# A row LSTM: output gates written to the next row's place of h, the odd cell tanh and product over 128 rows, and no copy of x rows into PSUM

## The chip, the cores and the metric

The kernel runs on one core of a Trainium2 chip. The metric is the device time of one execution, in microseconds (us); for the kernel before it is the median of three runs.

## The reference

The input `x` is (8, 96, 128, 128): 8 images, 96 channels, 128 rows of 128 pixels. It is normalised over groups of 3 channels (mean and variance over 3 x 128 x 128), and the normalised image goes through a convolutional LSTM that walks down the rows:

```python
its = conv(X, W_is * mask, 1x3) + b_is        # 4*96 outputs for each pixel, all rows at once
def step(carry, row_in):                       # one row of 8 images x 128 pixels
    h, c = carry
    gates = conv1d(h, W_ss, 3 taps) + b_ss + row_in
    f, i, o = sigmoid(...), sigmoid(...), sigmoid(...); g = tanh(...)   # 96 channels each
    c_new = f * c + i * g
    h_new = o * tanh(c_new)
    return (h_new, c_new), h_new
out = x + hs
```

The mask leaves two of the three taps of `W_is` (the pixel to the left and, for part of the channels, the pixel itself). Everything is 32-bit float. Row r needs h and c of row r - 1, so the 128 rows are a chain.

## The kernel before

Until about 155 us the kernel reads all of x once for the sums of the normalisation, while the first rows start. The rest, which this document is about, is the walk down the rows.

**Half-steps.** The 8 images are two groups of four (s = 0 and 1). A *half-step* `n` is one row of one group; the groups alternate, so the work of two half-steps overlaps. There are 256 half-steps; 252 of them are written by one string, `PERIOD`, that lists the work of all engines in order. The scheduler is switched off for TensorE (PE), ScalarE (ACT), VectorE (DVE) and GpSimd (POOL): each engine runs its own part of that string in that order, and waits with semaphores where it needs something. A name in the string is an operation, the letter behind it a bank or a pixel kind, `'` the half-step before, `+` the one behind.

**Pixels.** Even pixels (part `a` in the string) and odd ones (`b`) are kept apart: a tile has 64 even and 64 odd pixels for each of four images, 256 columns each. `hx[s][i][:, r]` holds a row: partitions 0 to 95 are h of the row before (the convolution's input), partitions 96 to 127 are 32 channels of the normalised x of this row, so one matmul over 128 partitions does both. A convolution of three taps over pairs of pixels is written with fewer products, from four operands: the sum `vs` of even and odd pixels (`total`, L750), their difference `vf` (`difference`, L754), and the differences of neighbours `vo` (`shifted_odd`, L764) and `ve` (`shifted_even`, in the tile `te`, L760).

**Banks and lanes.** A half-step has three PSUM banks of 128 x 512: A (forget gate, and a third of g), B (input gate, and a third of the output gate), C (two thirds of the output gate and two of g). Columns 0 to 255 are first the part `m` that both pixel kinds share, columns 256 to 511 the part that differs. When the shared part is complete, ScalarE copies it with the bias to SBUF (`copy`, L629); VectorE makes the even gates `m + differing` (`even`, L635) and the odd ones `m - differing` (`odd`, L639), and the rest of the products (`vo`, `te`) is added on top. Every product is cut into two matmuls over 64 partitions (two *lanes*, partitions 0 to 63 and 64 to 127), which run beside each other; where both lanes write one bank, an empty instruction on TensorE (`Lanes.wait`) lets the second wait for the first. TensorE shows two instructions for a 32-bit matmul.

**The gates and h.** ScalarE makes tanh of g (`tanh`, L644), sigmoid of the gates (`sigmoid`, L665), and the last third of the output gate (`last_output_gate`, `o2`, L670), which lies in partitions 96 to 127 of bank B. Output gates go to a tile `o` of 96 x 512. VectorE multiplies input gate and g for odd pixels (`gated`, L684; GpSimd does the even ones, L682), forget gate and c (`forget`, L675), and adds both to c (`cell`, L697). ScalarE takes tanh of c (`cell_tanh`, L705) to PSUM: odd pixels to bank B, even ones to bank C. VectorE multiplies with `o` (`output`, L714): the even h goes to its place in `hx` of the next row; the odd h stays in PSUM, in bank B's columns 256 to 511, partitions 0 to 95. Three things read the odd h there: `total` and `difference` of the next row, `residual` (L776, out = x + h), and a copy on ScalarE to `hx` (`keep_odd`, `co`, L725), from which GpSimd makes `vo`. Since `total` and `difference` need 128 partitions, ScalarE first copies the 32 odd x rows of the next row out of `hx` into partitions 96 to 127 of the same columns (`shared_odd`, `uo`, L730):

```python
self.kept["uo"] = nc.scalar.activation(
    self.odd_output[C:P], hx[self.s][i][C:P, r, 1, :, 1 : J + 1], AF.Identity
)
```

PSUM is tracked by whole banks; where two instructions touch different partitions of a bank, `apart` tells the framework that they need not wait for each other.

## Time and profile before

| | |
|---|---|
| median of 3 runs | 1937.43 us (1936.2 to 1940.31) |
| the profiled execution | 1935.68 us, its span 1933.9 us |
| mean granted TensorE clock | 0.990 |
| busy share of the span: PE, ACT, DVE, POOL | 97%, 86%, 81%, 81% |
| the chain that ended last | PE 92%, DMA 3%, DVE 2%, ACT 1%, POOL 1% |
| from 190 to 1904 us | 15663 matmul instructions in 1714 us |

An execution's time holds its span and what lies around it. A line of the profile names the source line, the engine, the operation, and output<-inputs by the program's names; `x2` behind it means that two equal ones were merged; what stands in brackets is the idle time ahead and who ended it. An instruction can start before the one ahead on its engine has ended, so durations of neighbours overlap.

### The profile page before, as it was taken

How to read it: one execution, taken by the hardware profiler on the slowest of the kernel's cores; microseconds unless marked ns; L12 is line 12 of the kernel's file. 1: busy time of each engine (PE TensorE's matmuls, PEld its weight loads, DVE VectorE, ACT ScalarE, POOL GpSimd, SP SyncE). 2: the span in 40 equal slices, each digit the busy share in tenths (PEclk: the TensorE clock that was granted, in tenths of full speed). 3: DMA queues.
4: the chain of work that ended last, by engine and by line, in shares of the span. 5: the costliest groups of instructions: out<-in, count | busy, mean ns of one | idle time of the engine just before them, and what ended most of it. 6: DMA issues, size and time to landing. Idle time of an engine off the chain costs nothing.

```text
span 1933.9 us, 45949 instructions
## 1 busy us (share of the span) xinstructions
PE 1876.7 (97%) x16440; PEld 1760.7 (91%) x16440; DVE 1565.7 (81%) x4024; ACT 1661.7 (86%) x3939; POOL 1566.5 (81%) x2172
## 2 busy tenths in 40 slices
PE   4789999999999999999999999999999999999998
PEld 1458999999999999999999999999999999999996
DVE  5887888888888888888888888888888888888886
ACT  6578888888888888888888888888888888888887
POOL 4348988888888888888888888888888888888852
PEclk8899999999999999999999999999999999999999
DMA  9995434433443443444344434443443444345311
GB/s 404 406 324 115 109 90 121 123 102 97 123 109 93 112 126 102 103 117 118 91 107 121 112 100 110 121 102 94 121 122 95 105 121 110 89 118 126 91 29 44
DMA packets 110292, 242.82 MB, mean 126 GB/s; under 512 B 6833, under 2 KB 16369, under 8 KB 104049
## 3 DMA queue, kind: packets, MB, share of 16 engines
q1 hardware_dynamic: 110064, 239.89, 45.1%
q8 instruction: 130, 2.13, 0.5%
q14 instruction: 98, 0.79, 0.1%
HBM read 181.34 MB, written 50.33 MB: 120 GB/s over the span
## 4 chain that ended last, share of the span: by engine, by line
PE 92%; DMA 3%; DVE 2%; ACT 1%; POOL 1%; issue 0%; SPq 0%; DVEq 0%; POOLq 0%; ACTq 0%
PE ps L553 92%; DMA x<-in_x_dram 2%; DVE bst L1229 1%; DMA te<-in_x_dram 1%; POOL xw L354 0%; ACT g L644 0%; POOL xs L375 0%; ACT ps L665 0%; PE rows L225 0%; POOL xs L371 0%; PE pv L308 0%; ACT o L670 0%; POOL g L682 0%; SPq L1216 0%; ACT hx L273 0%
## 5 line engine op out<-in xcount | busy, mean ns | idle before, releaser
L553 PE MATMUL ps<-te,wl 64*128 64x256 f32 (+1 forms) x3042 | 924.3, 384 | 0.2
L553 PE MATMUL ps<-vf,wm 64*128 64x256 f32 (+1 forms) x3046 | 780.5, 376 | 0.1
L553 PE MATMUL ps<-vo,wl 64*128 64x256 f32 (+1 forms) x3042 | 736.1, 384 | 2.5 <-DVE ps L639 2.4
L553 PE MATMUL ps<-xs,wx 64*128 64x256 f32 (+1 forms) x3080 | 731.1, 377 | 3.4 <-POOL xs L371 2.3
L553 PE MATMUL ps<-vs,wm 64*128 64x256 f32 (+1 forms) x3046 | 676.8, 376 | 2.9 <-DVE vs L750 2.8
L635 DVE TENSOR_TENSOR ps<-m,ps 128x256 f32<-128x256 f32 x768 | 323.4, 421 | 266.7 <-ACT m L629 266.6
L553 PEld LDWEIGHTS ps<-te,wl 64*128 64x128 f32 (+1 forms) x3042 | 511.9, 185 | 29.9 <-PE ps L553 1.4
L553 PEld LDWEIGHTS ps<-vo,wl 64*128 64x128 f32 (+1 forms) x3042 | 495.5, 186 | 13.9 <-issue 4.0
L553 PEld LDWEIGHTS ps<-xs,wx 64*128 64x128 f32 x3080 | 492.3, 187 | 15.3 <-POOL xs L371 3.2
L553 PEld LDWEIGHTS ps<-vs,wm 64*128 64x128 f32 (+1 forms) x3046 | 452.9, 187 | 14.3 <-DVE vs L750 4.2
L553 PEld LDWEIGHTS ps<-vf,wm 64*128 64x128 f32 (+1 forms) x3046 | 446.5, 185 | 16.1 <-PE ps L553 0.9
L629 ACT ACTIVATE m<-ps,wl 128x256 f32<-128x256 f32 x766 | 359.9, 470 | 23.2 <-PE ps L553 10.4
L644 ACT ACTIVATE g<-ps 32x512 f32<-32x512 f32 x765 | 317.8, 447 | 55.1 <-PE ps L553 39.8
L639 DVE TENSOR_TENSOR ps<-m,ps 128x256 f32<-128x256 f32 x768 | 325.5, 424 | 17.6
L553 PE MATMUL ps<-xs,wt 64*128 64x256 f32 x1012 | 299.2, 376 | 1.4 <-DVE ps L639 1.4
L682 POOL TENSOR_TENSOR g<-i,g 96x256 f32<-96x256 f32 x251 | 182.2, 726 | 144.3 <-ACT g L644 143.7
L375 POOL TENSOR_TENSOR xs<-xw 128x512 f32<-128x512 f32 (+1 forms) x254 | 293.2, 1155 | 0.1
L665 ACT ACTIVATE ps<-ps 96x512 f32<-96x512 f32 (+1 forms) x512 | 243.2, 475 | 34.9 <-PE ps L553 12.0
L354 POOL TENSOR_SCALAR xw<-xr,rstd,nmr 128x512 f32<-128x512 f32 (+1 forms) x267 | 208.2, 781 | 37.3 <-DVE nmr L346 13.0
L705 ACT ACTIVATE ps<-c 96x256 f32<-96x256 f32 x512 | 193.2, 378 | 39.7 <-DVE c L697 4.6
L354 POOL TENSOR_SCALAR hx<-x,rstd,nmr 32x512 f32<-32x512 f32 x248 | 201.6, 813 | 25.7
L697 DVE TENSOR_TENSOR c<-ps,g 96x256 f32<-96x256 f32 (+1 forms) x507 | 211.2, 417 | 10.1 <-POOL g L682 1.3
(133 smaller groups left out, 2608.5 us busy)
## 6 DMA issues: line engine op xcount, KB each, us to landing
xr<-in_x_dram SPq DMA_DIRECT2D x124, 512.0 KB, 6.6
x<-in_x_dram SPq DMA_DIRECT2D x62, 768.0 KB, 5.2
out_dram<-x SPq DMA_DIRECT2D x62, 768.0 KB, 4.6
x<-in_x_dram SPq DMA_DIRECT2D x16, 1024.0 KB, 11.0
x<-in_x_dram SPq DMA_DIRECT2D x62, 256.0 KB, 3.0
xs<-in_x_dram SPq DMA_DIRECT2D x15, 1024.0 KB, 11.1
te<-in_x_dram SPq DMA_DIRECT2D x8, 1024.0 KB, 10.3
hx<-in_x_dram SPq DMA_DIRECT2D x8, 1024.0 KB, 9.6
```

The source lines that it names most:

```text
L354: return engine.tensor_scalar(dst, src, scale, shift, ALU.mult, ALU.add)
L375: return engine.tensor_sub(differences, strided(xw[:, 0, :], 0, [(W + 1, n), (J + 1, 2), (1, J)]), strided(xw[:, 0, :], J, [(W + 1, n), (0 ...
L553: made = nc.tensor.matmul(self.ps[a][:, bass.ts(half, HB)][:, cols], weights[rows, bass.ts(a, P)], rhs[rows, cols], start=new, stop=False, ...
L629: made = nc.scalar.activation(self.m1[a], m1, AF.Identity, bias=column)
L635: nc.vector.tensor_add(self.ps[a][:, 0:HB], self.m1[a], self.ps[a][:, HB:])
L639: nc.vector.tensor_sub(hi, self.m1[a], hi)
L644: made = nc.scalar.activation(self.part(g, lo, hi, t), self.part(ps, lo, hi, t), AF.Tanh)
L665: made = nc.scalar.activation(to, gate, AF.Sigmoid)
L682: nc.gpsimd.tensor_mul(to, i, g)
L697: nc.vector.tensor_add(c, f, g)
L705: nc.scalar.activation(th, self.part(self.c, lo, hi, t), AF.Tanh)
L1229: nc.vector.bn_stats(bst[:, done, :], xc[:, bass.ts(j, SN)])
```

## The change

- `sigmoid` of bank C and `last_output_gate` write the output gates to the next row's place of h in `hx` (`self.h`, partitions 0 to 95, even and odd pixels) instead of the tile `o`, which is gone. The product for even pixels replaces the gate in place; `keep_odd` later writes the odd h over the odd gate.
- c becomes 128 partitions high; partitions 96 to 127 of its odd half are filled once with 30.0, whose tanh is 1. The odd `cell_tanh` and the odd `output` run over 128 partitions. There the second factor is what lies in partitions 96 to 127 of the next row's `hx`: the normalised x. So the product leaves h and x beside each other in PSUM.
- `shared_odd` is gone, and so is its `uo'` in `PERIOD`, in `LAST` and in the half-step 1.
- The bookkeeping of `apart` becomes a general rule (`touch`). The dependency that held the copy of bank B behind a product of bank C (`"2C"`) is gone. `do` takes one more mark in names that `PERIOD` doesn't use; `LAST` names one residual more, of a half-step that is done by then.

```diff
-    cs = [const.tile([C, 2, BH, J], F32, tag=f"c{s}", name=f"c{s}") for s in range(NH)]
+    cs = [const.tile([P, 2, BH, J], F32, tag=f"c{s}", name=f"c{s}") for s in range(NH)]
...
+        nc.gpsimd.memset(cs[s][C:P, 1], 30.0)
...
+            nxt = hx[self.s][(self.row + 1) // R % 2][:, (self.row + 1) % R]
+            self.beside = strided(nxt[:, 0, 0, :], 0, [(BH * JP + 1, 2), (JP, BH), (1, J)])
+            self.h = self.beside[0:C]
+            self.wide = P if self.banked and self.row + 1 < NT else C
...
+        def touch(self, a, made, lo, hi):
+
+            before = self.touched.setdefault(a, [])
+            same = made.ins.engine == E.Activation
+            for other, l, h, at in before:
+                if (h <= lo or l >= hi) and (
+                    other.ins.engine != made.ins.engine or same and at < len(activations) - 1
+                ):
+                    apart(made, other)
+            before.append((made, lo, hi, len(activations)))
+            return made
...
-                made = nc.scalar.activation(self.m1[a], m1, AF.Identity, bias=column)
-                if a == order["B"] and "2C" in self.kept:
-                    follow(made, self.kept["2C"], "the products of this bank end ahead of it")
+                activate(self.m1[a], m1, AF.Identity, bias=column)
...
             elif a == order["C"]:
-                to = self.part(self.o[0:C2], lo, hi, t)
+                to = self.h[0:C2, :, lo:hi] if t is None else self.h[0:C2, t, lo:hi]
...
         def last_output_gate(self):
-            self.kept["o2"] = nc.scalar.activation(self.o[C2:C], self.ps[1][C:P], AF.Sigmoid)
+            made = activate(self.h[C2:C], self.part(self.ps[1][C:P], 0, BH), AF.Sigmoid)
+            self.touch(1, made, C, P)
...
         def tanh_of(self, t):
-            return self.ps[(2, 1)[t]][0:C]
+            return self.ps[(2, 1)[t]][0 : self.wide if t else C]
...
             for t in range(2) if t is None else (t,):
                 th = self.part(self.tanh_of(t), lo, hi, t)
-                nc.scalar.activation(th, self.part(self.c, lo, hi, t), AF.Tanh)
+                of = self.c_or_one[0 : self.wide] if t else self.c
+                made = activate(th, self.part(of, lo, hi, t), AF.Tanh)
+                self.touch((2, 1)[t], made, 0, self.wide if t else C)
...
             for t in range(2) if t is None else (t,):
-                o, th = (self.part(ap, lo, hi, t) for ap in (self.o, self.tanh_of(t)))
-                to = th if t == 1 and self.banked else self.h[:, t, lo:hi]
-                made = nc.vector.tensor_mul(to, o, th)
-                if t == 1 and self.banked:
-                    self.kept["oub"] = made
-                    apart(made, self.kept.get("uo"))
+                th, wide = self.part(self.tanh_of(t), lo, hi, t), self.wide if t else C
+                o = self.beside[0:wide, t, lo:hi]
+                to = th if t == 1 and self.banked else o
+                self.touch((2, 1)[t], nc.vector.tensor_mul(to, o, th), 0, wide)
...
-        def shared_odd(self):
-            if self.banked and self.row + 1 < NT:
-                i, r = (self.row + 1) // R % 2, (self.row + 1) % R
-                self.kept["uo"] = nc.scalar.activation(
-                    self.odd_output[C:P], hx[self.s][i][C:P, r, 1, :, 1 : J + 1], AF.Identity
-                )
-                apart(self.kept["uo"], self.kept.get("gtb"), self.kept.get("oub"))
...
-        "ceb' 1C> rea'' loB thb' cea' QA+< hiB tha' 3A> 0B< oub' uo' oua' 0A> EB< QC+> cpC S' "
+        "ceb' 1C> rea'' loB thb' cea' QA+< hiB tha' 3A> 0B< oub' oua' 0A> EB< QC+> cpC S' "
```

On TensorE and on the DMA queue of SyncE the order and the waits stay as they were in all 252 half-steps; GpSimd has the two fills more, at the start. VectorE runs the same operations in the same order. Here it is from the odd difference of bank B to that of bank C, in row 61 of group 1 with bank C of row 63 of group 0 (`ps1` is bank B, `ps2` bank C, `hx11` the place of the next row). Before:

```order
L639 TENSOR_TENSOR ps1_0_63_11856<-m1_0_63_11942,ps1_0_63_11856 128x256 [waits DVE_49]
L714 TENSOR_TENSOR ps1_1_61_11766<-o_1_61_11915,ps1_1_61_11766 96x256 [waits Activation_49]
L714 TENSOR_TENSOR hx11_70<-o_1_61_11915,ps2_1_61_11794 96x4x64 [waits Activation_49]
L750 TENSOR_TENSOR vs_1_62_11980<-hx11_70,ps1_1_61_11766 128x256 [waits DVE_49,Activation_49]
L754 TENSOR_TENSOR vf_1_62_11982<-ps1_1_61_11766,hx11_70 128x256
L635 TENSOR_TENSOR ps2_0_63_11884<-m2_0_63_11978,ps2_0_63_11884 128x256 [waits Activation_49]
L639 TENSOR_TENSOR ps2_0_63_11884<-m2_0_63_11978,ps2_0_63_11884 128x256 [waits DVE_49]
```

And now:

```order
L662 TENSOR_TENSOR ps1_0_63_11613<-m1_0_63_11697,ps1_0_63_11613 128x256 [waits DVE_49]
L729 TENSOR_TENSOR ps1_1_61_11525<-hx11_70,ps1_1_61_11525 128x256 [waits Activation_49]
L729 TENSOR_TENSOR hx11_70<-hx11_70,ps2_1_61_11552 96x4x64 [waits Activation_49]
L755 TENSOR_TENSOR vs_1_62_11734<-hx11_70,ps1_1_61_11525 128x256 [waits DVE_49]
L759 TENSOR_TENSOR vf_1_62_11736<-ps1_1_61_11525,hx11_70 128x256
L658 TENSOR_TENSOR ps2_0_63_11640<-m2_0_63_11732,ps2_0_63_11640 128x256 [waits Activation_49]
L662 TENSOR_TENSOR ps2_0_63_11640<-m2_0_63_11732,ps2_0_63_11640 128x256 [waits DVE_49]
```

The two products read `hx11` where they read `o`, the first over 128 partitions; the sum behind them (L750, now L755) waits for VectorE alone, no longer for VectorE and ScalarE.

ScalarE in the same half-step, from the output gates of bank C to the last third of the output gate of the next half-step. Before:

```order
L665 ACTIVATE o_1_61_11915<-ps2_1_61_11794 64x512
L705 ACTIVATE ps1_1_61_11766<-c1_82 96x256 [waits DVE_49]
L705 ACTIVATE ps2_1_61_11794<-c1_82 96x256 [waits DVE_49,Activation_49]
L730 ACTIVATE ps1_1_61_11766<-hx11_70 32x256
L629 ACTIVATE m2_0_63_11978<-ps2_0_63_11884,wl_61 128x256 [waits PE_49]
L665 ACTIVATE ps0_0_63_11853<-ps0_0_63_11853 96x512 [waits PE_49]
L725 ACTIVATE hx11_70<-ps1_1_61_11766 96x4x64 [waits DVE_49,Activation_49]
L644 ACTIVATE g_0_63_11998<-ps0_0_63_11853 32x512 [waits Activation_49,Pool_49]
L670 ACTIVATE o_0_63_12004<-ps1_0_63_11856 32x512 [waits PE_49]
L665 ACTIVATE i_0_63_12008<-ps1_0_63_11856 96x256
```

And now (all activations are issued by one helper, so they share a line):

```order
L520 ACTIVATE hx11_70<-ps2_1_61_11552 64x2x4x64
L520 ACTIVATE ps1_1_61_11525<-c1_82 128x256 [waits DVE_49]
L520 ACTIVATE ps2_1_61_11552<-c1_82 96x256 [waits DVE_49,Activation_49]
L520 ACTIVATE m2_0_63_11732<-ps2_0_63_11640,wl_61 128x256 [waits PE_49]
L520 ACTIVATE ps0_0_63_11610<-ps0_0_63_11610 96x512 [waits PE_49]
L520 ACTIVATE hx11_70<-ps1_1_61_11525 96x4x64 [waits DVE_49]
L520 ACTIVATE g_0_63_11752<-ps0_0_63_11610 32x512 [waits Pool_49]
L520 ACTIVATE hx00_67<-ps1_0_63_11613 32x2x4x64 [waits PE_49]
L520 ACTIVATE i_0_63_11761<-ps1_0_63_11613 96x256
```

The copy of the x rows (32x256, L730) is gone, and the copy of `m2`, the shared part of bank C, follows the two tanh directly. The gates go to `hx11` and `hx00`, in four runs of 64 for each pixel kind. The copy of the odd h and the tanh behind it have each lost the wait on ScalarE itself.

More of the change, by code (lines that the diff above doesn't have):

```diff
@@ L513, with activate @@
     whole = slice(0, P)
+    activations = []
+    def activate(*args, **kwargs):
+        activations.append(nc.scalar.activation(*args, **kwargs))
+        return activations[-1]
     class HalfStep:
@@ L520, in __init__ @@
             i, r = self.row // R % 2, self.row % R
-            self.ps, self.m1, self.done, self.gates, self.outputs = {}, {}, set(), None, None
+            self.ps, self.m1, self.done, self.gates = {}, {}, set(), None
             self.banked = self.n >= 1
@@ L643, in tanh @@
             g, ps = self.g[to], self.ps[a][of]
-            made = nc.scalar.activation(self.part(g, lo, hi, t), self.part(ps, lo, hi, t), AF.Tanh)
-            if a == order["A"]:
-                self.kept["taA"] = made
-        @property
-        def o(self):
-            if self.outputs is None:
-                self.outputs = self.tile("o")
-            return self.outputs
+            made = activate(self.part(g, lo, hi, t), self.part(ps, lo, hi, t), AF.Tanh)
+            self.touch(a, made, of.start, of.stop)
         def sigmoid(self, a, lo=0, hi=BH, t=None):
@@ L661, in sigmoid @@
             elif a == order["C"]:
-                to = self.part(self.o[0:C2], lo, hi, t)
+                to = self.h[0:C2, :, lo:hi] if t is None else self.h[0:C2, t, lo:hi]
             else:
                 to = gate
-            made = nc.scalar.activation(to, gate, AF.Sigmoid)
+            made = activate(to, gate, AF.Sigmoid)
+            self.touch(a, made, 0, C2 if a == order["C"] else C)
             if a == order["C"] and self.banked and (self.row + 1) % R == 0 and self.s in widened:
@@ L674, in forget @@
             if self.row > 0:
-                apart(nc.vector.tensor_mul(f, f, c), self.kept.get("taA"))
+                self.touch(0, nc.vector.tensor_mul(f, f, c), 0, C)
         def gated(self, lo=0, hi=BH, t=None):
@@ L775, in residual @@
                 engine = nc.gpsimd if t == 0 and self.n < last else nc.vector
-                engine.tensor_add(xo[:, t], xo[:, t], h)
+                made = engine.tensor_add(xo[:, t], xo[:, t], h)
+                if t == 1 and self.banked:
+                    self.touch(1, made, 0, C)
                 return
@@ L915, in do @@
         for name in names.split():
-            if name == "U":
-                prepare(n - 1, name)
-                continue
-            if name[0] == "W":
-                prepare(n - 1 + name.count("+") - name.count("'"), name.strip("W+'"))
+            if name[0] in "UW":
+                ahead = name.count("+") + 2 * name.count("*") - name.count("'")
+                prepare(n - 1 + ahead, name.strip("W+*'"))
                 continue
@@ L1292 @@
     finish(0)
[L1293 removed]
+    do(1, "gt th 0+A 3+A 0+B 3+B 0+C 3+C ou co F S D0 D1 re")
     finish(1)
```

23 lines of the change are left out of this document (9 added, 14 removed), and 2 rows, old and new, of the table PARTS.

## The prediction

> **What bounds the kernel now.** I read the page's busy shares first, then stretches of the span, then the timelines of one half-step, and the waits last. The page says that TensorE is busy nearly always:
>
> ```profile
> PE 1876.7 (97%) x16440; PEld 1760.7 (91%) x16440; DVE 1565.7 (81%) x4024; ACT 1661.7 (86%) x3939; POOL 1566.5 (81%) x2172
> ```
>
> That hides the question. The busy times by stretch answer it. The columns are the stretch, its length, then for PE, PEld, DVE, ACT and POOL the busy time and the number of instructions, then the granted clock:
>
> ```profile
> 190.00:1904.00 1714.00, 1714.00 (x15663) 1653.73 (x15663) 1403.51 (x3670) 1510.87 (x3671) 1459.35 (x1939) 1.00 0.42 106
> 1000.25:1003.70 3.45, 3.45 (x35) 3.38 (x33) 3.31 (x11) 3.11 (x9) 3.13 (x5) 1.00 0.72 142
> 1003.70:1007.25 3.55, 3.55 (x35) 3.38 (x33) 2.44 (x7) 3.07 (x9) 2.90 (x5) 1.00 0.18 37
> ```
>
> In the middle 1714 us the matmul row has no idle time at all, and the clock is 1.00. The next two rows are the two halves of one half-step. Each has 35 matmuls, of which three were still running from before, so 32 begin in each; but 32 beginnings take 3.45 us in the first half and 3.55 us in the second. A half-step has 64 of them and takes 7.00 us; at the pace of the first half it would take 2 x 3.45 = 6.90. So TensorE loses 0.10 us somewhere in each half-step, although no view calls it idle. With 15663 / 64 = 244.7 half-steps in the stretch (1714 / 244.7 = 7.004 us each), all that could be won here is about 244.7 x 0.10 = 24 us.
>
> The Trainium skill ("Trainium Kernel Development and Optimization", Performance Expectations) calls matmul busy time a bad metric and weight-load busy time a good one. By the first there is nothing to win. By the second there is: the PEld column has 1653.73 of 1714. The trace sides with the second.
>
> TensorE's timeline shows where the loss is:
>
> ```profile
> 1003.71 0.80 PE L553 MATMUL ps<-vo,wl 64*128 64x256 f32 x4
> ...
> 1004.34 0.38 PE L553 MATMUL ps<-te,wl 64*128 64x256 f32 x1
> 1004.36 0.38 PE L553 MATMUL ps<-vf,wm 64*128 64x256 f32 x1
> ...
> 1006.39 0.70 PE L553 MATMUL ps<-xs,wx 64*128 64x256 f32 x4
> ```
>
> Matmuls come from two row groups in turn, which run beside each other; I call them lanes. Four in a row at full pace take 0.70 us (the last row). The four odd products of bank C from 1003.71 take 0.80, and behind them the two lanes start 0.02 us apart (1004.34, 1004.36) where they would alternate by 0.108 (3.45 / 32). One lane came 0.10 late. Its products need VectorE's difference for bank C, so I go there:
>
> ```profile
> 1001.36 0.42 DVE L714 TENSOR_TENSOR ps<-o,ps 96x256 f32<-96x256 f32 x1
> 1001.69 0.41 DVE L714 TENSOR_TENSOR hx<-o,ps 96x256 f32<-96x256 f32 x1
> 1002.20 0.42 DVE L750 TENSOR_TENSOR vs<-hx,ps 128x256 f32<-128x256 f32 x1
> 1002.54 0.42 DVE L754 TENSOR_TENSOR vf<-ps,hx 128x256 f32<-128x256 f32 x1
> 1002.87 0.42 DVE L635 TENSOR_TENSOR ps<-m,ps 128x256 f32<-128x256 f32 x1
> 1003.32 0.43 DVE L639 TENSOR_TENSOR ps<-m,ps 128x256 f32<-128x256 f32 x1
> ...
> 1005.72 0.43 DVE L635 TENSOR_TENSOR ps<-m,ps 128x256 f32<-128x256 f32 x1 [1.05 <-ACT m L629]
> 1006.18 0.43 DVE L639 TENSOR_TENSOR ps<-m,ps 128x256 f32<-128x256 f32 x1
> 1006.57 0.42 DVE L684 TENSOR_TENSOR g<-ps,g 96x256 f32<-96x256 f32 x1
> 1007.02 0.42 DVE L697 TENSOR_TENSOR c<-ps,g 96x256 f32<-96x256 f32 x1
> ```
>
> The `L639` at 1003.32 is that difference. It ends at 1003.75, and the late lane starts behind it. From 1006.57 on VectorE does not rest until the next one at 1010.32 (the same rows 7.00 us later): an instruction that needs nothing from the one ahead starts 0.33 us after it (1001.36 to 1001.69), one that waits for the result ahead starts 0.03 after that ends (1005.72 + 0.43 = 6.15, then 6.18; 1006.57 + 0.42 = 6.99, then 7.02; 1002.87 + 0.42 = 3.29, then 3.32). One breaks the pattern: `L750`, the sum of even and odd pixels, starts at 1002.20, while the product ahead ended at 1001.69 + 0.41 = 2.10. That is 0.10 instead of 0.03.
>
> ScalarE in the same half-step (`L730` is the copy of x rows into PSUM):
>
> ```profile
> 1000.68 0.90 ACT L705 ACTIVATE ps<-c 96x256 f32<-96x256 f32 x2
> 1001.61 0.38 ACT L730 ACTIVATE ps<-hx 32x256 f32<-32x256 f32 x1
> 1002.01 0.48 ACT L629 ACTIVATE m<-ps,wl 128x256 f32<-128x256 f32 x1
> 1002.61 0.57 ACT L665 ACTIVATE ps<-ps 96x512 f32<-96x512 f32 x1
> 1003.10 0.37 ACT L725 ACTIVATE hx<-ps 96x256 f32<-96x256 f32 x1
> ...
> 1004.34 0.59 ACT L670 ACTIVATE o<-ps 32x512 f32<-32x512 f32 x1 [0.24 <-PE ps L553]
> ...
> 1006.16 0.65 ACT L644 ACTIVATE g<-ps 64x256 f32<-64x256 f32 x2 [0.20 <-PE ps L553]
> 1006.83 0.47 ACT L629 ACTIVATE m<-ps,wl 128x256 f32<-128x256 f32 x1
> ```
>
> ```profile
> DVE ps L635 <- ACT m L629: 258.1, 244, 1.1
> ...
> ACT o L670 <- PE ps L553: 59.0, 241, 0.2
> ...
> ACT g L644 <- PE ps L553: 38.1, 184, 0.3
> ```
>
> Two chains lead into VectorE's stretch. **Chain 1:** bank C's last products release the tanh `L644` at 1006.16 (idle 0.20 before it, for PE); its first half lasts 0.38, and VectorE's `L684` starts behind it at 1006.57. This chain closes on itself: late difference for C, late lane, late tanh, `L684`, next difference. From 1003.75 to 1010.75 it is 7.00 us, and I find no link with slack. **Chain 2:** bank B's products release `L670` at 1004.34, ScalarE makes the copy that VectorE's `L635` at 1005.72 waits for (the first line of the waits: 258.1 us in 244 pieces), and `L639` at 1006.18 would let `L684` start at 6.18 + 0.33 = 6.51. It starts at 6.57, so chain 2 has 0.06 us of slack. It closes over two half-steps: bank B's last products run in the other lane, which waits for the late one only behind them, so they feel a delay one half-step later.
>
> **The change, part by part.** *The copy of x rows goes.* It is `L730`, 0.38 us and 0.02 us of turnaround per half-step (1001.61 to 1002.01): 252 x 0.40 = 101 us of ScalarE. On its own that is worth nothing. The copy `L629` behind it moves up at most to 1001.61, but `L635`, which needs it at 1002.87, has time since 2.01 + 0.48 = 2.49. The sigmoid `L665` at 1002.61 has 0.12 us of idle time ahead and waits for TensorE, so it stays, and with it everything on ScalarE until `L670`, which waits again.
>
> *What goes with it is a wait.* The sum `L750` waits now for VectorE's product and for ScalarE's copy; after the change for the product alone. I take the row 0.03 (three dependent starts with one wait) for its new gap, so it starts 0.10 - 0.03 = 0.07 us earlier, and the difference for C behind it too. The bounds are 0, if the 0.10 has another cause, and 0.10, if the lane's whole loss goes. The copy `L725` and the tanh behind it lose a wait each, too; `L725` starts at the pace of the sigmoid ahead (1002.61 to 3.10), `L670` waits for PE: nothing.
>
> The Trainium skill ("VectorE: DVE Perf Modes", The DRAIN you can't avoid) says the opposite: eight copies with a semaphore after each and with one after the last took the same time, so a semaphore costs nothing extra. By that the gain would be 0. The rows 0.03 and 0.10 above differ by a second wait on one instruction, which that measurement did not have.
>
> What 0.07 us is worth: chain 1 would close in 7.00 - 0.07 = 6.93. Chain 2 closes in (2 x 7.00 - 0.06 - 0.07) / 2 = 6.935. But chain 2 is not the same in each half-step:
>
> ```profile
> 738.34 0.59 ACT L670 ACTIVATE o<-ps 32x512 f32<-32x512 f32 x1 [0.24 <-PE ps L553]
> ...
> 745.40 0.59 ACT L670 ACTIVATE o<-ps 32x512 f32<-32x512 f32 x1 [0.25 <-PE ps L553]
> ...
> 752.34 0.59 ACT L670 ACTIVATE o<-ps 32x512 f32<-32x512 f32 x1 [0.25 <-PE ps L553]
> ...
> 766.40 0.59 ACT L670 ACTIVATE o<-ps 32x512 f32<-32x512 f32 x1 [0.25 <-PE ps L553]
> ```
>
> `L670` comes 0.06 late at 745.40 (7.06 after the one ahead, then 6.94) and again at 766.40; that is two of eight half-steps, and chain 2's slack swallows it today. Once chain 2 binds, it costs 2 x 0.06 / 8 = 0.015 per half-step. So the half-step is 6.935 + 0.015 = 6.95, **0.05 us less, and 244.7 x 0.05 = 12.2 us**. VectorE's pace allows it (its idle 1.05 us before `L635` moves with the chain), TensorE's too (6.90).
>
> *At both ends* the copy stands on the chain that ended last, with nothing beside it:
>
> ```profile
> 152.81 0.39 ACT ps L730
> ```
> ```profile
> 1918.61 0.39 ACT ps L730
> ```
>
> 0.39 us and the 0.02 of turnaround, once at the start and once near the end: 0.8 us.
>
> *Output gates into h's place, odd tanh and product over 128 rows.* By form:
>
> ```profile
> L705 ACT ACTIVATE ps<-c 96x256 f32<-96x256 f32 x512 | 193.2, 378 | 39.7 <-DVE c L697 4.6 <-DVE ps L639 0.4 <-DVE c L684 0.2
> ...
> L670 ACT ACTIVATE o<-ps 32x512 f32<-32x512 f32 x256 | 151.1, 590 | 61.9 <-PE ps L553 61.8
> ...
> L730 ACT ACTIVATE ps<-hx 32x256 f32<-32x256 f32 x252 | 95.8, 380 | 6.3
> ...
> L725 ACT ACTIVATE hx<-ps 96x256 f32<-96x256 f32 x252 | 93.9, 373 | 0.9 <-DVE ps L714 0.5 <-DVE ps L635 0.2
> ...
> L352 ACT ACTIVATE hx<-x,nmr,rstd 32x512 f32<-32x512 f32 x4 | 3.4, 845 | 9.7 <-DVE nmr L346 9.6
> ```
>
> More rows cost nothing: 96 rows take 378 ns (`L705`), 32 rows 380 (`L730`). Nor should the place: `L725` writes 256 elements to h's place in 373. For the two gate sigmoids (512 elements over both pixel kinds) no row shows it; the nearest are that one, cost 0, and `L352`, which writes 512 to the same layout and takes 845 against 590 for `L670`: 0.255 more, though it also reads SBUF at a step of two pixels and takes its scale from memory. Bounds 0 and 0.255 for each; I take 0, by `L725`, which also reads PSUM and writes the same rows. The gate of bank C has cover: the first tanh of the cell behind it (1000.68, 0.38 long) ends at 1001.06, and the product that needs it starts at 1001.36, so 0.27 us are free; past that it adds to chain 1. The gate `L670` has no cover but chain 2's slack. The products now read strided rows; `L750` does so in 0.42 as they do in 0.42 and 0.41, so 0, or 0.01 at most. The dropped order of bank B's copy behind the products of C is nothing: that copy starts at 1006.83, after a tanh that waited for C. The two fills of 30.0 lie before the first load has landed.
>
> Sum, against the profiled run's 1935.68 us (span 1933.9 and 1.8 around it): 12.2 + 0.8 = 13.0, so 1922.7. The median of the three runs shown, 1937.43, is 1.75 higher: **1924.4 us**, or -0.67%.
>
> **Rivals.** *The gap is not the wait's* (or chain 2 does not move): the half-step stays at 7.00, and only the 0.8 us at the ends are won: 1936.6. For it: the skill's rule, and that `L750` is the only instruction of its kind here to judge by. Against: three dependent starts with one wait at 0.03 each. *All of the loss goes:* if the late `L670` of two in eight does not count and both chains fall under TensorE's pace, the half-step is 6.90 and 244.7 x 0.10 + 0.8 = 25 us go: 1912. For it: 0.07 of 0.10 goes by my own sum; against: chain 2's half share. *Slower:* the strided write costs `L670` x us. Chain 2 then closes in 6.95 + x / 2, and from x = 0.10 on it is slower than now. At `L352`'s 0.255 it is 7.08, 0.08 x 244.7 = 19 us longer, with the ends 1955. For it: `L352` is ScalarE's only row with 512 elements into this layout; against: `L725`. That the change does not remove what it says is excluded by the order of instructions.
>
> **How the numbers follow.** Forecast 0.59, no gain 0.16, all of the loss 0.14, slower 0.11. A measurement tells 0.2%, 4 us, from no change here. Faster is 0.59 + 0.14 = 0.73, the same 0.16, slower 0.11. The forecast's own range is 1918 (0.07 us in full) to 1931 (half of it). To leave out no more than 2 in 10 I go from 1913, close to the case in which all of the loss goes, to 1938, which holds the case of no gain.
>
> **What would show it.** Right: the sum starts 0.03 us behind the end of the product instead of 0.10; 32 matmuls of the second half take 3.50 instead of 3.55 and the half-step 6.95; chain 2 has no slack left, so `L684` starts 0.33 us behind `L639` where it is 0.39 now (6.18 to 6.57); ScalarE has 100 us less busy time and all of it as idle. Wrong: the sum starts 0.10 after, in which case the wait was not the cause; or the gate sigmoids last longer than 0.60 us; or the period stays at 7.00 with the sum earlier, in which case a third chain binds that I have not seen.

## The result, and the profile after

The changed kernel takes **1926.69 us** (median of 4 runs, 1925.03 to 1928.97) against 1938.87 us for the kernel before on the same chip (4 runs, 1936.20 to 1940.41): a ratio of 0.9939, 95% interval 0.9922 to 0.9957. Forecast were 1924.4 us and a ratio of 0.9933. Later runs gave 1927.12 against 1937.09, a ratio of 0.9946 (0.9932 to 0.9960). The profiled execution took 1926.39 us, its span 1924.6 us, 9.3 less than before.

Busy times of the page, after:

```profile
PE 1870.1 (97%) x16440; PEld 1747.4 (91%) x16440; DVE 1556.1 (81%) x4024; ACT 1564.0 (81%) x3687; POOL 1567.7 (81%) x2174
```

ScalarE has 97.7 us less to do (1661.7 before), TensorE's share is 97% as before. The page doesn't show where the 9.3 us went. The stretches do (the same columns as before; the second and third row are the two halves of one half-step):

```profile
190.00:1896.00 1706.00, 1706.00 (x15662) 1639.68 (x15660) 1394.44 (x3670) 1416.02 (x3427) 1459.47 (x1939) 1.00 0.42 106
1002.62:1006.07 3.45, 3.45 (x36) 3.39 (x33) 3.38 (x11) 2.67 (x8) 3.07 (x5) 1.00 0.00 0
1006.07:1009.59 3.52, 3.52 (x36) 3.33 (x34) 2.31 (x7) 3.12 (x8) 2.96 (x5) 1.00 0.00 0
```

15662 matmuls are 244.7 half-steps; they now take 1706.00 us where they took 1714, so a half-step takes 6.972 us instead of 7.004. That is 244.7 x 0.032 = 7.8 us of the 9.3; the other 1.5 lie outside this stretch. TensorE's first half has kept its 3.45, the second has gone from 3.55 to 3.52, where 3.50 was expected.

VectorE's stretch, after (`L662` is an odd difference, first of bank A, at 1005.70 of bank C; `L702` the product of input gate and g; `L729` the two products with the output gate; `L755` the sum, `L759` the difference, `L658` the even gates):

```profile
1001.68 0.43 DVE L662 TENSOR_TENSOR ps<-m,ps 128x256 f32<-128x256 f32 x1
1002.02 0.41 DVE L702 TENSOR_TENSOR g<-ps,g 96x256 f32<-96x256 f32 x1
1002.47 0.42 DVE L712 TENSOR_TENSOR c<-ps,g 96x256 f32<-96x256 f32 x1
1002.81 0.42 DVE L658 TENSOR_TENSOR ps<-m,ps 128x256 f32<-128x256 f32 x1
...
1003.80 0.42 DVE L729 TENSOR_TENSOR ps<-hx,ps 128x256 f32<-128x256 f32 x1
1004.13 0.41 DVE L729 TENSOR_TENSOR hx<-hx,ps 96x256 f32<-96x256 f32 x1
1004.57 0.42 DVE L755 TENSOR_TENSOR vs<-hx,ps 128x256 f32<-128x256 f32 x1
...
1005.70 0.43 DVE L662 TENSOR_TENSOR ps<-m,ps 128x256 f32<-128x256 f32 x1
```

The sum starts at 1004.57, and the product ahead ended at 1004.13 + 0.41 = 4.54: 0.03 instead of 0.10. And `L702` starts 0.34 behind the odd difference of A (1001.68 to 1002.02), where the same two stood 0.39 apart before. This is VectorE's own pace (0.33 to 0.34 from start to start where nothing is waited for), so chain 2 has no slack left.

What the second wait was can be seen when the instructions of that one line are grouped (duration in ns: least, median, most; first and last start in us; `DVEq` is VectorE's queue, for instructions that compute nothing). Before:

```profile
L750 DVE TENSOR_TENSOR vs<-hx,ps x252: 404/422/422, 153.6 to 1920.1; 128x256 f32<-128x256 f32 x126
L750 DVEq EVENT_SEMAPHORE  x250: 21/21/21, 160.5 to 1905.6; - x125
```

After:

```profile
L755 DVE TENSOR_TENSOR vs<-hx,ps x252: 407/421/422, 152.7 to 1910.8; 128x256 f32<-128x256 f32 x126
```

Before, 250 of the 252 sums had an instruction of their own in VectorE's queue that only waited, 21 ns long; after, none has.

ScalarE by form, before (`L665` is the gate sigmoid of bank C; that of bank B, `L670`, is in the prediction):

```profile
L665 ACT ACTIVATE o<-ps 64x512 f32<-64x512 f32 x256 | 148.1, 579 | 0.1
```

After (first and second row: the gates of banks B and C at their new place; third: the odd tanh over 128 rows):

```profile
L520 ACT ACTIVATE hx<-ps 32x512 f32<-32x512 f32 x256 | 151.5, 592 | 63.6 <-PE ps L578 63.5
...
L520 ACT ACTIVATE hx<-ps 64x512 f32<-64x512 f32 x256 | 148.2, 579 | 0.1
...
L520 ACT ACTIVATE ps<-c 128x256 f32<-128x256 f32 x252 | 93.6, 371 | 0.1
```

592 ns for 590, 579 for 579, and 128 rows in 371 where 96 take 378. The product over 128 rows takes 0.42 us (1003.80) as it did over 96. On ScalarE and VectorE the place costs nothing.

### The profile page after: what moved, and what is told of

The parts are those of the page before. It is cut to its first block, busy times and chain, and to the rows that moved or that the text cites. A ratio compares the mean times of both kernels' runs of the same rounds, so it can differ in the third digit from the quotient of the medians.

```text
span 1924.6 us, 45262 instructions
## 1 busy us (share of the span) xinstructions
PE 1870.1 (97%) x16440; PEld 1747.4 (91%) x16440; DVE 1556.1 (81%) x4024; ACT 1564.0 (81%) x3687; POOL 1567.7 (81%) x2174
## 4 chain that ended last, share of the span: by engine, by line
PE 92%; DMA 3%; DVE 2%; ACT 1%; POOL 1%; issue 0%; SPq 0%; DVEq 0%; POOLq 0%; ACTq 0%
PE ps L578 91%; DMA x<-in_x_dram 1%; DMA te<-in_x_dram 1%; DVE bst L1234 1%; PE rows L226 1%; POOL xw L355 0%; ACT g L520 0%; ACT ps L520 0%; POOL xs L376 0%; POOL xs L372 0%; ACT hx L520 0%; ACT x L274 0%; ACT x L275 0%; PE pv L309 0%; POOL g L700 0%
## 5 line engine op out<-in xcount | busy, mean ns | idle before, releaser
L578 PE MATMUL ps<-te,wl 64*128 64x256 f32 (+1 forms) x3042 | 903.1, 377 | 0.2
L578 PE MATMUL ps<-vo,wl 64*128 64x256 f32 (+1 forms) x3042 | 727.9, 382 | 2.5 <-DVE ps L662 2.5
L578 PE MATMUL ps<-xs,wx 64*128 64x256 f32 (+1 forms) x3080 | 698.9, 377 | 0.6 <-DVE c L712 0.2
L578 PE MATMUL ps<-vs,wm 64*128 64x256 f32 (+1 forms) x3046 | 645.7, 377 | 2.1 <-DVE vs L755 1.9
L578 PEld LDWEIGHTS ps<-te,wl 64*128 64x128 f32 (+1 forms) x3042 | 536.8, 186 | 27.6 <-PE ps L578 1.4
L658 DVE TENSOR_TENSOR ps<-m,ps 128x256 f32<-128x256 f32 x768 | 323.5, 422 | 285.5 <-ACT m L520 285.4
L578 PEld LDWEIGHTS ps<-vo,wl 64*128 64x128 f32 (+1 forms) x3042 | 480.6, 186 | 12.4 <-issue 3.5
L578 PEld LDWEIGHTS ps<-vf,wm 64*128 64x128 f32 (+1 forms) x3046 | 457.9, 185 | 32.2 <-PE ps L578 0.9
L520 ACT ACTIVATE hx<-ps 96x256 f32<-96x256 f32 (+1 forms) x764 | 393.8, 515 | 64.4 <-PE ps L578 63.5
L578 PEld LDWEIGHTS ps<-vs,wm 64*128 64x128 f32 (+1 forms) x3046 | 435.7, 187 | 6.8 <-DVE vs L755 3.4
L662 DVE TENSOR_TENSOR ps<-m,ps 128x256 f32<-128x256 f32 x768 | 325.7, 425 | 17.6
L520 ACT ACTIVATE ps<-c 96x256 f32<-96x256 f32 (+1 forms) x512 | 193.0, 377 | 47.1 <-DVE c L712 44.5
## 6 DMA issues: line engine op xcount, KB each, us to landing
xs<-in_x_dram SPq DMA_DIRECT2D x15, 1024.0 KB, 12.2
```

What stands on the lines that cost most here:

```text
L520: activations.append(nc.scalar.activation(*args, **kwargs))
L578: made = nc.tensor.matmul(self.ps[a][:, bass.ts(half, HB)][:, cols], weights[rows, bass.ts(a, P)], rhs[rows, cols], start=new, stop=False, ...
L658: nc.vector.tensor_add(self.ps[a][:, 0:HB], self.m1[a], self.ps[a][:, HB:])
L662: nc.vector.tensor_sub(hi, self.m1[a], hi)
```

## The experiments

Eleven variants were run, and the changed kernel once more, each against the kernel before on the same chip. The half-step is the mean interval between two sums from 190 to 1890 us. In the edits, `...` stands for lines left out; where an edit adds a wait, they only keep GpSimd's instruction under the name (`rea`, `te` or `xs`) that the shown lines wait for.

| kernel | us (runs) | ratio to before (95%) | half-step, us |
|---|---|---|---|
| before | 1937.09 to 1938.87, by chip | 1 | 7.004 |
| changed | 1926.69 (4) | 0.9939 (0.9922 to 0.9957) | 6.973 |
| changed, again | 1927.12 (5) | 0.9946 (0.9932 to 0.9960) | 6.973 |
| sum waits twice | 1936.50 (12) | 0.9992 (0.9983 to 1.0001) | 7.012 |
| difference waits once | 1926.97 (6) | 0.9942 (0.9929 to 0.9954) | 6.973 |
| a copy nobody reads | 1926.48 (6) | 0.9943 (0.9929 to 0.9956) | 6.971 |
| new place of the gates alone | 1937.03 (12) | 0.9998 (0.9987 to 1.0009) | 7.010 |
| odd A waits twice | 1936.80 (10) | 0.9988 (0.9974 to 1.0003) | 7.013 |
| odd C waits twice | 1938.24 (10) | 1.0002 (0.9992 to 1.0012) | 7.015 |
| odd A and odd C | 1946.14 (9) | 1.0038 (1.0026 to 1.0050) | 7.047 |
| sum and odd C | 1959.55 (4) | 1.0107 (1.0088 to 1.0125) | 7.083 |
| lanes in another order | 1963.15 (4) | 1.0128 (1.0114 to 1.0143) | 7.108 |
| difference behind the even gates | 1945.17 (5) | 1.0046 (1.0032 to 1.0060) | 7.049 |
| both of these | 1978.66 (4) | 1.0218 (1.0204 to 1.0233) | 7.189 |

**The wait alone, given back.** The changed kernel, in which the sum waits for a second engine again, for something that was done long ago:

```diff
-            engine.tensor_add(self.operand("vs")[:, 0, lo:hi], e, o)
+            made = engine.tensor_add(self.operand("vs")[:, 0, lo:hi], e, o)
+            late = steps.get(self.n - NH - 1)
+            if self.n > NH + 1 and late is not None and "rea" in late.kept:
+                follow(made, late.kept["rea"], "one wait more")
...
+                if t == 0 and engine is nc.gpsimd:
+                    self.kept["rea"] = made
```

> The changed kernel, but VectorE's sum of even and odd pixels waits for one thing more: GpSimd's residual of a half-step before, which ended about 0.8 us earlier, so nothing is waited for, there is only a second wait on the instruction. No copy of x rows comes back. Theory (the gain is the second wait that left the sum): the sum starts 0.10 us behind the product instead of 0.03, the half-step is back at 7.00 us, and the time is 1926.7 + 245 x 0.03 = 1934 (within 2 us). Rival (the gain is ScalarE's 100 us less of work): half-step 6.97, 1927.

Its instructions of that line, grouped as above:

```profile
L755 DVEq EVENT_SEMAPHORE  x249: 21/21/21, 169.8 to 1909.9; - x125
```

and VectorE's timeline in it:

```profile
1005.06 0.41 DVE L729 TENSOR_TENSOR hx<-hx,ps 96x256 f32<-96x256 f32 x1
1005.57 0.42 DVE L755 TENSOR_TENSOR vs<-hx,ps 128x256 f32<-128x256 f32 x1
```

The waiting instruction is back, the sum starts 1005.57 - (1005.06 + 0.41) = 0.10 behind the product's end, and the time is 1936.50: the whole gain is gone, with ScalarE's copy still away. So the wait was the gain. What arrives late there is nothing; having two waits costs the 0.07. The half-step is 7.012, 0.012 more than was expected, and the time 0.5 us beyond the expected bounds: in this kernel the product starts 0.34 behind odd A (1002.60 to 1002.94 in its timeline), so here chain 2 binds, where chain 1 did in the kernel before.

**The same wait on the next instruction**, the difference, which has none of its own (it follows the sum on the same engine and reads what the sum has read):

```diff
-            engine.tensor_sub(self.operand("vf")[:, 0, lo:hi], o, e)
+            made = engine.tensor_sub(self.operand("vf")[:, 0, lo:hi], o, e)
+            late = steps.get(self.n - NH - 1)
+            if self.n > NH + 1 and late is not None and "rea" in late.kept:
+                follow(made, late.kept["rea"], "one wait more")
...
```

> The same extra wait for the same GpSimd instruction, but on the next VectorE instruction, the difference of odd and even pixels, which has no other wait. Theory (what costs is a second wait on one instruction that depends on the one ahead, not a wait as such): the difference starts 0.34 us behind the sum as before, half-step 6.97, 1927. Rival (each satisfied wait costs some 0.07 us of VectorE's time): half-step 7.00, 1934.

```profile
1003.75 0.41 DVE L729 TENSOR_TENSOR hx<-hx,ps 96x256 f32<-96x256 f32 x1
1004.19 0.42 DVE L755 TENSOR_TENSOR vs<-hx,ps 128x256 f32<-128x256 f32 x1
1004.53 0.42 DVE L759 TENSOR_TENSOR vf<-ps,hx 128x256 f32<-128x256 f32 x1
```

In this timeline of VectorE the sum keeps its 0.03 (1003.75 + 0.41 to 1004.19), the difference starts 0.34 behind it, as without the wait, and the time is 1926.97. A single wait that is already met costs nothing. That agrees with the Trainium skill ("VectorE: DVE Perf Modes", The DRAIN you can't avoid), by which a semaphore costs nothing extra. For an instruction that waits for its neighbour's result and for a second engine as well, which that page's measurement did not have, the 1936.50 above shows that the rule doesn't hold.

**ScalarE's copy alone, given back**, into a tile that nobody reads:

```diff
+        def spare_copy(self):
+            if self.banked and self.row + 1 < NT:
+                i, r = (self.row + 1) // R % 2, (self.row + 1) % R
+                activate(unread_rows[C:P], hx[self.s][i][C:P, r, 1, :, 1 : J + 1], AF.Identity)
...
-        "ceb' 1C> rea'' loB thb' cea' QA+< hiB tha' 3A> 0B< oub' oua' 0A> EB< QC+> cpC S' "
+        "ceb' 1C> rea'' loB thb' cea' QA+< hiB tha' 3A> 0B< oub' uo' oua' 0A> EB< QC+> cpC S' "
...
```

> The changed kernel with ScalarE's copy of the 32 odd x rows put back in its old place, but into a tile that nobody reads, so no instruction waits for it. Theory (ScalarE's work there lies under its wait for TensorE): half-step 6.97, 1927, ScalarE 96 us busier than in the changed kernel. Rival (the gain is ScalarE's work): half-step 7.00, 1934 or more.

```profile
PE 1869.8 (97%) x16440; PEld 1747.6 (91%) x16440; DVE 1555.4 (81%) x4024; ACT 1667.1 (87%) x3938; POOL 1567.8 (82%) x2174
```

ScalarE is as busy as before the change (1667.1 us, 87%), and the time is 1926.48. The 98 us that ScalarE no longer works are worth nothing.

**The new place of the gates alone.** Tanh and product over 96 rows, and the copy of x rows into PSUM, as before the change; the gates stay in h's place:

```diff
-            self.wide = P if self.banked and self.row + 1 < NT else C
+            self.wide = C
...
+        def shared_odd(self):
+            if self.banked and self.row + 1 < NT:
+                i, r = (self.row + 1) // R % 2, (self.row + 1) % R
+                made = activate(
+                    self.odd_output[C:P], hx[self.s][i][C:P, r, 1, :, 1 : J + 1], AF.Identity
+                )
+                self.touch(1, made, C, P)
...
-        "ceb' 1C> rea'' loB thb' cea' QA+< hiB tha' 3A> 0B< oub' oua' 0A> EB< QC+> cpC S' "
+        "ceb' 1C> rea'' loB thb' cea' QA+< hiB tha' 3A> 0B< oub' uo' oua' 0A> EB< QC+> cpC S' "
...
```

> One part of the change alone: the output gates go to the next row's place of h, but the odd tanh and product run over 96 partitions and the copy of x rows into PSUM stays, and with it the second wait on the sum. Theory (the place of the gates costs nothing): half-step 7.00, and as long as the kernel before, 1938 (within 2 us); the two gate sigmoids take 0.59 and 0.58 us as before. Rival (gates written in runs of 64 cost something, which the whole change hides): longer than the kernel before, by 245 x half of what the last third of the output gate takes more.

```profile
L763 DVEq EVENT_SEMAPHORE  x250: 21/21/21, 158.4 to 1905.0; - x125
```

The sum has its waiting instruction (250 of 252), and the time is that of the kernel before, 1937.03, ratio 0.9998. So this part of the change neither costs nor brings anything in time that the runs can tell (its half-step is 7.010); it is there because the wider product needs it.

**Which chain binds.** The changed kernel loses 0.032 per half-step by a saving of 0.07. By the prediction, chain 1 would now close in 6.93 and chain 2, over two half-steps, in about 6.95; the trace says 6.97. A second wait is a delay of known size that can be put on one chain or on both. Odd A stands on chain 2 alone, odd C and the sum on both. Odd A first:

```diff
-            nc.vector.tensor_sub(hi, self.m1[a], hi)
+            made = nc.vector.tensor_sub(hi, self.m1[a], hi)
+            late = steps.get(self.n - 3)
+            if a == order["A"] and late is not None and "rea" in late.kept:
+                follow(made, late.kept["rea"], "one wait more")
...
```

> The changed kernel, whose odd difference of bank A (the one ahead of the odd product of input gate and g) waits also for GpSimd's residual of three half-steps before, which was done some 5 us earlier. It waited for VectorE's even gates alone. Nothing else changes. This instruction stands on chain 2 alone (copy A, even A, odd A, product), not on chain 1, which enters VectorE behind it through the tanh of C. Theory (a second wait costs 0.07 us on any dependent instruction of VectorE; chain 2 binds at 6.973 and closes over two half-steps): the gap between the even and the odd gates of A grows from 0.03 to 0.10, the half-step is 6.973 + 0.07 / 2 = 7.008, 245 x 0.035 = 8.6 us: 1935.5. Rival, the price belongs to the sum alone: 1927. Rival, chain 1 binds: 1927 to 1928, although the gap has grown. Rival, a delay of VectorE counts in full: 7.043 and 1944.

VectorE's timeline in it (`L658` even A, `L662` odd A, `L705` the product behind it):

```profile
1004.23 0.43 DVE L658 TENSOR_TENSOR ps<-m,ps 128x256 f32<-128x256 f32 x1 [1.07 <-ACT m L520]
1004.77 0.43 DVE L662 TENSOR_TENSOR ps<-m,ps 128x256 f32<-128x256 f32 x1
1005.11 0.41 DVE L705 TENSOR_TENSOR g<-ps,g 96x256 f32<-96x256 f32 x1
```

The gap ahead of odd A is 4.77 - (4.23 + 0.43) = 0.11 instead of 0.03, and the half-step has grown by 0.040, about half of it. So the price isn't the sum's alone, and a delay that only chain 2 has counts by half: chain 2 closes over two half-steps, and it binds.

Odd C in the same way (`self.n - 2` and `order["C"]` in the edit above):

> The changed kernel, whose odd difference of bank C waits also for GpSimd's residual of two half-steps before, which was done some 2 us earlier. It waited for VectorE's even gates alone. This instruction stands on both chains. Theory: the gap between the even and the odd gates of C grows from 0.03 to 0.10; chain 1, which has about 0.03 us of slack at 6.973, goes to 7.01, chain 2 to 6.973 + 0.07 / 2 = 7.008; the time is that of the kernel whose sum waits twice, 1936. Rival, the price belongs to the sum alone: 1927. Rival, chain 1 has no slack: 7.043 and 1944.

It gave 1938.24 and 7.015, about as with the sum (7.012).

Then two second waits in each half-step, on odd A (for GpSimd's difference of even neighbours) and odd C:

```diff
+            late = steps.get(self.n - 2)
+            if a == order["C"] and late is not None and "rea" in late.kept:
+                follow(made, late.kept["rea"], "one wait more")
+            if a == order["A"] and "te" in self.kept:
+                follow(made, self.kept["te"], "one wait more")
...
```

> The changed kernel with a second wait on two instructions: the odd difference of bank A (for GpSimd's difference of neighbours of even pixels, done 1.4 us earlier) and that of bank C (for the residual). Chain 1 has one of them, chain 2 both. Theory: chain 1 closes in 6.94 + 0.07 = 7.01, chain 2 in 6.973 + (0.07 + 0.07) / 2 = 7.043, which binds: 245 x 0.07 = 17 us, 1944. Rival, each second wait costs a like amount wherever it stands: the same as in the run with sum and odd C. Rival, the price belongs to the sum alone: 1927.

or on the sum (as in the first experiment) and odd C (for GpSimd's subtraction of pixels):

```diff
+            if a == order["C"] and "xs" in recent:
+                follow(made, recent["xs"], "one wait more")
...
```

> The changed kernel with a second wait on two instructions that both chains hold: the sum (for GpSimd's residual, done 0.8 us earlier) and the odd difference of bank C (for GpSimd's subtraction of pixels, done 0.8 us earlier). Theory: chain 2 closes in 7.043 as in the run with odd A and odd C, but chain 1 in 6.94 + 2 x 0.07 = 7.08, and chain 1 binds: 245 x 0.107 = 26 us, 1953. Rival, each second wait costs a like amount, or chain 2 alone decides: 1944, the same as with odd A and odd C. Rival, the price belongs to the sum alone: 1936.5.

Odd A and the product behind it in VectorE's timeline, with odd A and odd C delayed:

```profile
1003.63 0.43 DVE L662 TENSOR_TENSOR ps<-m,ps 128x256 f32<-128x256 f32 x1
1003.97 0.41 DVE L707 TENSOR_TENSOR g<-ps,g 96x256 f32<-96x256 f32 x1
```

with the sum and odd C delayed:

```profile
1005.62 0.43 DVE L666 TENSOR_TENSOR ps<-m,ps 128x256 f32<-128x256 f32 x1
1006.01 0.42 DVE L708 TENSOR_TENSOR g<-ps,g 96x256 f32<-96x256 f32 x1
```

The same number of second waits gives a half-step of 7.047 in one place and 7.083 in the other. The times differ by more, 1946.14 and 1959.55: 245 x 0.036 = 9 us of these 13 are the half-step's. Most of the rest seems to be lost before the walk, where an odd difference of the second kernel really had to wait for GpSimd:

```profile
96.78 0.43 DVE L666 TENSOR_TENSOR ps<-m,ps 128x256 f32<-128x256 f32 x1 [6.12 <-POOL xs L377]
```

Its first sum of the walk comes at 157.7, that of the first kernel at 152.7; that would explain why 1959.55 is longer than the 1953 that was expected, although the half-step is the expected one (7.08). So the half-steps are compared here, not the times. In the first the product still starts 0.34 behind odd A: chain 2 binds, and two waits at half their price make 7.047 - 6.973 = 0.074, so 0.074 each (the gaps show 0.07). In the second it starts 0.39 behind, as in the kernel before: odd A has slack again, chain 1 binds. With 0.074 for each wait, chain 1 without them is 7.083 - 2 x 0.074 = 6.935, with 0.07 it is 6.943. The forecast for it was 6.93. So the half-steps fit both chains as described: in the changed kernel chain 1 closes in about 6.94, chain 2 in 6.973. With one delay on both they meet (6.935 + 0.074 = 7.009, 6.973 + 0.037 = 7.010), so the times with the sum or odd C alone could not tell them apart.

**Three attempts to win more**, the first also meant to test chain 2's way through TensorE (the section below shows its rows). First, on TensorE, a product of bank B ahead of one of the next half-step's own products, so that the late lane would meet the other one later:

```diff
-        "siBb' 2C< taCb' U loA taCa' hiA cpB siC' PA+> gtb' QB+< 2C> 0A< PB+> 3A< PC> EA< gta' "
+        "siBb' 2C< 2B> taCb' U loA taCa' hiA cpB siC' gtb' QB+< 2C> 0A< PB+> 3A< PC> EA< gta' "
...
-        "D0' W2+ 1B+< 3C> fg reb' 2B+< 0C> 1C+< cpA+ 2B+>"
+        "D0' W2+ 1B+< 3C> fg reb' 2B+< 0C> 1C+< cpA+ PA*>"
```

> The changed kernel with two neighbours on TensorE swapped: the even-and-odd product of bank A with x of the half-step after goes ahead of the second lane's difference product of bank B, which is the one that waits for the other lane. Theory (half-step 6.97 instead of my 6.95, because the late lane now reaches the other one by this wait, 0.06 us later on its way than by the wait of bank C): with the wait one product later chain 2 loses those 0.06, half-step 6.94, 1919. Rival (the 0.02 us are something else): half-step 6.97, 1927.

It became slower, 1963.15. ScalarE's timeline (the tanh of C, and the copy of bank B):

```profile
1006.32 0.65 ACT L520 ACTIVATE g<-ps 64x256 f32<-64x256 f32 x2 [0.19 <-PE ps L578]
1007.18 0.47 ACT L520 ACTIVATE m<-ps,wl 128x256 f32<-128x256 f32 x1 [0.21 <-PE ps L578]
```

and VectorE's (the first cell sum, and the even gates of B):

```profile
1007.18 0.42 DVE L712 TENSOR_TENSOR c<-ps,g 96x256 f32<-96x256 f32 x1
1007.69 0.43 DVE L658 TENSOR_TENSOR ps<-m,ps 128x256 f32<-128x256 f32 x1
```

The edit puts the second lane of that product later, not earlier, and bank B's copy on ScalarE now waits 0.21 us for it. The copy ends at 7.65, VectorE's even gates of B start at 7.69, 0.51 behind the cell sum instead of 0.34 (1002.47 to 1002.81 in the changed kernel). This is another wait than the one meant, so the run says nothing on the lanes.

Second, VectorE's difference behind the even gates of C, so that odd C would find its even gates ready:

```diff
-        "F' siA W3 3B< co' loC hiC W1+ 1B+> 1A+< 2A+< 3B> 0B> 0C< taA 2A+> 3C< 1A+> o2 D1' siBa "
+        "siA W3 3B< loC F' co' hiC W1+ 1B+> 1A+< 2A+< 3B> 0B> 0C< taA 2A+> 3C< 1A+> o2 D1' siBa "
```

> The changed kernel with one VectorE instruction moved: the difference of odd and even pixels goes between the two of bank C, which depend on each other, instead of ahead of both. The odd difference of bank C then starts 0.33 us behind its neighbour where it had to wait 0.45, so it is 0.12 us earlier. Theory (VectorE's stretch up to that instruction sets the half-step, by half of what it gains on chain 2): half-step 6.91, TensorE's pace, 1912. Rival (the difference, now 0.33 us later, stalls TensorE in its place, or the copy of odd h behind it does): half-step 6.97 or longer, 1927 or more.

```profile
1005.59 0.42 DVE L658 TENSOR_TENSOR ps<-m,ps 128x256 f32<-128x256 f32 x1
1005.92 0.42 DVE L759 TENSOR_TENSOR vf<-ps,hx 128x256 f32<-128x256 f32 x1
1006.26 0.42 DVE L662 TENSOR_TENSOR ps<-m,ps 128x256 f32<-128x256 f32 x1
```

In this timeline of VectorE odd C does start 0.34 behind its neighbour (1005.92 to 1006.26). But the waits of this kernel (total us, times, longest) have a line that the changed kernel's do not:

```profile
PEld ps L578 <- DVE vf L759: 45.1, 241, 0.4
```

TensorE now waits for the difference, 0.19 us in each half-step, and the time is 1945.17. The place won on one operand is lost on the other. Third, both edits together:

> Both moves together. Theory: TensorE's own pace is the floor, half-step 6.91, 1912, no faster than the second move alone. Rival: the two gains add, half-step 6.88 or less, 1905.

1978.66: no gain, and the losses nearly add up (36 and 18 us over the changed kernel's 1927.12 alone, 52 together). No version is clearly faster than the changed kernel. The run that repeated it was there for the comparison:

> The changed kernel as it is, to stand beside the three others on one chip: 1927, half-step 6.97.

## Why the prediction was right, and where it was not

**What bounds the kernel: right.** TensorE's loss of 0.10 us per half-step, which no view calls idle, is now 0.07 (6.972 against 6.90), and the time went with the half-step, not with ScalarE's 98 us.

**The wait: right.** 0.10 became 0.03, the whole effect of the change can be undone with a wait alone, and none of it by giving the copy back. The rival in which the gap isn't the wait's falls with the first experiment, the slower one with the new place of the gates alone.

**Chain 1: right.** 6.93 forecast, 6.935 to 6.943 worked out from the run with the sum and odd C.

**Chain 2: mis-sized.** "6.935 + 0.015 = 6.95" was the term; it measured 6.973. The chain is the right one (the half price of a delay on odd A shows that), but it is longer than the sum had it. Cut the chain in two: from odd C to the gate sigmoid of bank B one half-step later, and from that sigmoid to the odd C of its own half-step. Before, to be read with 1003.32 and 1004.34 in the prediction:

```profile
1010.32 0.43 DVE L639 TENSOR_TENSOR ps<-m,ps 128x256 f32<-128x256 f32 x1
```

```profile
1011.34 0.59 ACT L670 ACTIVATE o<-ps 32x512 f32<-32x512 f32 x1 [0.24 <-PE ps L553]
```

After, to be read with odd C at 1005.70:

```profile
1012.68 0.43 DVE L662 TENSOR_TENSOR ps<-m,ps 128x256 f32<-128x256 f32 x1
```

```profile
1006.82 0.59 ACT L520 ACTIVATE hx<-ps 32x512 f32<-32x512 f32 x1 [0.25 <-PE ps L578]
...
1013.78 0.59 ACT L520 ACTIVATE hx<-ps 32x512 f32<-32x512 f32 x1 [0.25 <-PE ps L578]
```

Before, 1003.32 to 1011.34 is 8.02 and 1004.34 to 1010.32 is 5.98: 14.00 for two half-steps. After, 1005.70 to 1013.78 is 8.08 and 1006.82 to 1012.68 is 5.86: 13.94. On the engines' side 0.12 went, where 0.06 of slack and 0.07 of the wait were counted. On TensorE's side the link has grown by 0.06 (0.05 as the mean of all half-steps), and that the prediction did not see: it took TensorE's part as fixed but for the late sigmoid of two half-steps in eight.

That late sigmoid is the same 0.06, and TensorE's queue shows what goes with it. An empty instruction of `Lanes.wait` (L494 before, L495 after) can stand in that queue (`PEldq`) as an instruction of its own that only waits, 51 ns long. Before, over all the run, and from 730 to 770 us alone:

```profile
L494 PEldq EVENT_SEMAPHORE  x63: 51/51/51, 173.8 to 1883.8; - x63
```

```profile
L494 PEldq EVENT_SEMAPHORE  x2: 51/51/51, 742.4 to 763.4; - x2
```

After:

```profile
L495 PEldq EVENT_SEMAPHORE  x314: 51/51/51, 155.6 to 1900.4; - x157
```

Before, 63 of 252 half-steps have one, one in four. The two at 742.4 and 763.4 stand ahead of the two sigmoids that the prediction calls late, 745.40 and 766.40 (the link to the first is 8.07, from odd C at 737.33), and none stands between 1003.32 and 1011.34, where the link is 8.02. After, there are 251 more, one in each half-step, and what was late in one of four is late in nearly all. A link that is 0.06 longer in each half-step costs 0.03 on a loop of two: 6.935 + 0.03 = 6.965, close to the 6.973. (At that half price, two in eight would have been 0.0075, not 0.015.)

In TensorE's timeline the place can be seen, behind an instruction of L495 at 1008.2. After:

```profile
1006.19 0.69 PE L578 MATMUL ps<-vo,wl 64*128 64x256 f32 x4
...
1008.35 0.69 PE L578 MATMUL ps<-vf,wm 64*128 64x256 f32 x4
1008.83 0.64 PE L578 MATMUL ps<-xs,wx 64*128 64x256 f32 x4
```

The odd products of C, four in 0.80 before, take 0.69 at 1006.19: the loss that the prediction found is gone there. But the four differences of bank B at 1008.35 come 0.48 ahead of the next ones (1008.83). At this place four products took 0.43 before:

```profile
1005.96 0.70 PE L553 MATMUL ps<-vf,wm 64*128 64x256 f32 x4
```

(the next row, 1006.39, is in the prediction). It isn't the earlier difference that brings this. With the new place of the gates alone, where the sum still waits twice, line L495 counts 314 as well, and the link is 8.08 long:

```profile
1002.01 0.43 DVE L662 TENSOR_TENSOR ps<-m,ps 128x256 f32<-128x256 f32 x1
```

```profile
1010.09 0.59 ACT L520 ACTIVATE hx<-ps 32x512 f32<-32x512 f32 x1 [0.25 <-PE ps L578]
```

So the sentence ahead of the prediction that TensorE's waits stayed as they were in all half-steps is wrong. That kernel shares mainly three things with the changed one: the gates' place, the rule `touch`, and the dropped order of bank B's copy behind the products of C (`"2C"`). The lists of instructions point to the last: built with that order kept, the changed kernel's program has 63 of these instructions again, as before. That program has not been run. The run with the lanes in another order also counts 63, but has the other wait described above, so no run prices the instruction by itself, and that it is the cause of the longer link is read from the rows. If it is, keeping the order would bring some 245 x 0.03 = 7 us more; this is an estimate from the 0.06 above.

**The parts costed at nothing: right, but for one.** The copy, the writing of the gates (0 taken, 0.255 possible) and 128 rows cost nothing on ScalarE. The dropped order of bank B's copy was put at nothing because of what ScalarE does there; on TensorE it is the likely source of the 0.03.

**The ends: not told.** 0.8 us were forecast, and 9.3 - 7.8 = 1.5 are left between the two profiled executions. But the first sum of the walk comes anywhere from 151.5 (new place of the gates alone) to 155.9 (sum waits twice) in executions with the same work ahead of it, so neither number can be told from chance.

**The sum.** 12.2 + 0.8 = 13.0 us were forecast for the profiled execution, 9.3 came. The medians differ by 12.2 in the first comparison and by 10.0 in the second. That the first comes close to the forecast is chance: its interval reaches from 8 to 15 us. The step to be corrected is chain 2's: its TensorE link, taken as late in two half-steps of eight, is late in nearly all, so the half-step lost 0.032 where 0.05 was forecast.

## What to carry to other kernels

On an engine that runs dependent instructions back to back on the critical path, count the waits of each: one that waits for its neighbour and for a second engine, however long that one has been done, starts later than one that waits for the neighbour alone, and the gap between the end of one row and the start of the next shows it. Look for such gaps before looking at busy shares: 98 us of work taken from an engine off the path brought nothing, and 0.07 us on the path, 252 times, all there was. After a change, count the instructions that only wait in every engine's queue: here 250 went from VectorE's and 251 came to TensorE's. When a delay sits on several loops of different length, put a known delay on one and on the other; the slope (whole, or half for a loop over two steps) tells which binds.

## What the runs showed of the hardware

A second wait on a VectorE instruction that depends on the one ahead is an instruction of its own in the queue, 21 ns long, and puts the start 0.07 us later (0.10 behind the end ahead instead of 0.03), on a sum and on differences alike, even when the event waited for lies 0.8 to 5 us back. The same wait, alone on an instruction without another, costs nothing that can be measured. And the half-step answers to it by 0.04 for each, so long as the loop over two half-steps binds.

On TensorE, too, a wait can stand in the queue as an instruction of its own, here 51 ns long. In the kernel before, the link from odd C to the sigmoid of bank B takes 8.02 us without it (1003.32 to 1011.34) and 8.07 in the one half-step of four that has it (737.33 to 745.40); in the changed kernel, with one in each half-step, it takes 8.08 (1005.70 to 1013.78). No run changes that instruction alone.
